# Empty places of the neighbour lists get an index past the rows, and every indexed gather carries a bound that skips them

## The chip, the cores and the metric

The kernel runs on one core of a Trainium2 chip. The metric is the device time of one execution in microseconds (us). Before the change its median over 9 runs is 2172.87 us (2168.15 to 2176.95).

The core's engines are written as in the profile: PE is TensorE (matmuls; PEld its weight loads), DVE is VectorE, ACT is ScalarE, POOL is GpSimd, SP is SyncE. SP and ACT issue plain DMAs; POOL issues the gathers by index (DMA_INDIRECT). All of them run on the same 16 DMA engines.

## The reference

Input x is 8 x 2048 x 256 and adj is 2048 x 2048, both float32. adj is sparse: 18,432 of its 4,194,304 entries are not zero (9 in a row on average, more in the first rows than in the last), and the diagonal is always filled. Two layers are computed, each with a residual and a layer norm.

```python
# layer 0: graph convolution
A_norm = A + eye(n)
deg    = sum(A_norm, 0) + sum(A_norm, 1) - diagonal(A_norm)
dinv   = rsqrt(deg)
A_hat  = A_norm * dinv[:, None] * dinv[None, :]
agg    = einsum('nm,bmd->bnd', A_hat, x).reshape(-1, d)
h      = relu(batchnorm(agg @ W1.T + b1, g1, be1))
out    = batchnorm(h @ W2.T + b2, g2, be2)
x      = layernorm(x + out)
# layer 1: attention of 4 heads, only where adj is not zero
q, k, v = split(x @ W)
scores  = q k^T / 8 + where(adj == 0, -inf, 0)
x       = layernorm(x + softmax(scores) v)
```

## The kernel before

The 2048 rows are cut into 16 blocks of 128 (one row per partition). Block 0, and in layer 0 block 1 too, is computed densely with matmuls. For the other blocks the kernel builds neighbour lists from adj and works on gathered rows.

**Lists** (`list_steps`, lines 246 to 321). For block t, `LISTS[t]` gives two numbers, such as (8, 3). The first is the number of columns in which partition p holds a neighbour of its own row p. Rows with more neighbours than that put the surplus into the left-over columns (the second number), where a partition holds any edge of the block and also the number of the row that it belongs to. In all there are 131 columns of 128 places, 35 of them left-over. `val` is 2048 minus the neighbour's number, and 0 in an empty place. Line 306 turns it into `key` = 2048 - val, line 307 limits it to 2047, so an empty place names the last row, and line 308 writes it as the integer `idx`. For the left-over columns `qi1` is the row of the edge within the block plus 1, or 0 when empty; lines 309 to 312 make of it `idxq`, the row whose query is to be gathered. Lines 313 to 319 make `fidx`, the place of the value in adj taken as one flat column: row times 2048 plus key. `padb` is -2^40 for an empty place, so that its exponential is 0, and `weights` (line 335) multiplies the weight of an empty place by 0.

Counted from the inputs, 2,352 of the 16,768 places are empty: 1,014 in the columns of a partition's own row, spread over the partitions, and 1,338 of the 4,480 left-over places, always the last partitions of the last columns.

**Layer 0.** `gather_value` (line 326) gathers one adj value per place into a column of `av`, 115 times. `gather` (line 562) gathers 128 rows of `xs_d` (x scaled by dinv, all 8 batches, 8 KB a row) into a slot, called `e` in the profile, 115 times. Sixteen slots are shared with other data; `gather_ahead` issues up to ten gathers before the tile in work. Own-row columns are added up on DVE (lines 639 and 643), left-over columns on PE with a 128 x 128 weight matrix (line 652). Between them run the first linear layer (line 393) and the list building of later blocks. A second pass (lines 680 to 812) has the second linear layer and the batch norm statistics.

**Attention** (`attention`, line 879). Batches go in four pairs. For each pair a projection writes rows of keys and values (4,128 bytes for a pair) to `kv_d` and of queries to `q_d`. Then for each of the 131 columns (blocks 1 to 15) `gather` (line 1211) gathers 128 rows into `kg` (10 buffers) and, in left-over columns, 128 query rows of 2 KB into `qg` (5 buffers). `score` multiplies and sums on DVE (lines 1233, 1235), `exps` is on ACT (1244), `weigh_values` on DVE or ACT (1265, 1260), `add_up` on PE (1276). The finished block goes through `finish` (DVE, 1087 and 1089), `residual` (POOL, 1096) and the output norm: `out_root` (two small POOL instructions, lines 144 and 146, a pow), `out_shift` (DVE, 866), `emit` (ACT, then a store on SP).

The order of every engine's instructions is written out by hand: a loop over the 524 columns of all pairs issues the score of column n + 5, the addition of column n and the gather of column n + 10, and a table `later` hangs the steps of the next pair's projection and of the norms on column numbers. The first ten gathers of the attention are issued together, at column number -19, while the first projection ends. Everything on POOL stands in one queue: gathers, residual additions, the norms' pow and memsets.

Of the kernel before, what the change touches and what calls it, by code (L numbers as in the profile page):

```python
# [14 lines left out]
ALU = mybir.AluOpType  # L15
# [27 lines left out]
def tile_gcn_then_masked_attention(  # L43
# [15 lines left out]
    nc = tc.nc  # L59
    ENG = mybir.EngineType  # L60
    PSUM = bass.MemoryType.PSUM
    P = 128
    B, N, D = x.shape
# [51 lines left out]
    qi1 = cpool.tile([P, NEDGE], F32, name="qi1")  # L115
# [130 lines left out]
    def list_steps(t, psum, name):  # L246

        r, m, cap, e0 = ELL[t], 8 * ROUNDS[t], CAP[t], edge0[t]
        here = slice(t, t + 1)
        ell = slice(col0[t], col0[t] + r)  # L250
        left_over = slice(col0[t] + r, col0[t] + r + cap)
        cols = slice(col0[t], col0[t] + r + cap)
        edges = slice(e0, e0 + cap)

        def junk():
            return lists.tile([P, MAXNB], F32, name="junk", bufs=2)

        nc.vector.scalar_tensor_tensor(
            junk()[:, : m - r], nbx[:, t, r:m], 0.0, ones[:, : m - r],
            op0=ALU.is_gt, op1=ALU.mult, accum_out=cnt[:, here],  # L260
        )
        nc.vector.tensor_copy(val[:, ell], nbx[:, t, :r])
        nc.vector.tensor_scalar(
            over[:, 0, here], nbx[:, t, m - 1 : m], 0.0, None, op0=ALU.is_gt
        )
        yield
        yield
        ps = psum.tile([P, 1], F32, name=name)
        nc.tensor.matmul(ps, tri, cnt[:, here], start=True, stop=True)
        yield  # L270
        nc.vector.tensor_copy(nbx[:, t, MAXNB : MAXNB + 1], ps)
        nc.vector.tensor_add(end[:, here], cnt[:, here], nbx[:, t, MAXNB : MAXNB + 1])
        nc.vector.tensor_scalar(
            over[:, 1, here], end[:, here], float(cap * P), None, op0=ALU.is_gt
        )
        oh = lists.tile([P, WE], F32, name="oh")[:, : cap * P]
        nc.vector.tensor_scalar(
            oh, iota_e[:, : cap * P], nbx[:, t, MAXNB : MAXNB + 1], None, op0=ALU.is_ge
        )
        nc.vector.scalar_tensor_tensor(  # L280
            oh, iota_e[:, : cap * P], end[:, here], oh, op0=ALU.is_lt, op1=ALU.mult
        )
        yield
        yield
        pg = psum.tile([P, cap, MAXNB + 2 - r], F32, name=name)
        for i in range(cap):
            nc.tensor.matmul(
                pg[:, i, :], oh[:, i * P : (i + 1) * P], nbx[:, t, r:], start=True, stop=True
            )
        yield  # L290
        rank = lists.tile([P, cap], F32, name="rank")
        nc.vector.tensor_sub(rank, epos[:, :cap], pg[:, :, MAXNB - r])
        nc.vector.tensor_copy(qi1[:, edges], pg[:, :, MAXNB + 1 - r])
        nc.vector.tensor_scalar(qn1[:, edges], qi1[:, edges], -1.0, None, op0=ALU.mult)
        for i in range(cap):
            c = left_over.start + i
            nc.vector.scalar_tensor_tensor(
                junk()[:, : m - r], iota_r[:, : m - r], rank[:, i : i + 1], pg[:, i, : m - r],
                op0=ALU.is_equal, op1=ALU.mult, accum_out=val[:, c : c + 1],
            )  # L300
        nc.vector.tensor_scalar(
            padb[:, cols], val[:, cols], 0.0, MASKED, op0=ALU.is_equal, op1=ALU.mult
        )
        key = lists.tile([P, MAXNB], F32, name="key")[:, : r + cap]
        q = lists.tile([P, cap], F32, name="q")
        nc.vector.tensor_scalar(key, val[:, cols], -1.0, float(N), op0=ALU.mult, op1=ALU.add)
        nc.vector.tensor_scalar(key, key, float(N - 1), None, op0=ALU.min)
        nc.vector.tensor_copy(idx[:, cols], key)
        nc.vector.tensor_scalar(
            q, qi1[:, edges], 1.0, float(t * P - 1), op0=ALU.max, op1=ALU.add  # L310
        )
        nc.vector.tensor_copy(idxq[:, edges], q)
        nc.vector.scalar_tensor_tensor(
            fidx[:, ell], rowid[:, here].to_broadcast([P, r]), float(N), key[:, :r],
            op0=ALU.mult, op1=ALU.add,
        )
        nc.vector.scalar_tensor_tensor(
            fidx[:, left_over], q, float(N), key[:, r:], op0=ALU.mult, op1=ALU.add
        )
        nc.vector.tensor_scalar(wgt[:, ell], key[:, :r], rowid[:, here], None, op0=ALU.is_equal)  # L320
        nc.vector.tensor_tensor(wgt[:, left_over], key[:, r:], q, op=ALU.is_equal)

    adj_flat = adj.rearrange("n (m o) -> (n m) o", o=1)
    av = lists.tile([P, NCOL], F32, name="av")

    def gather_value(col):
        nc.gpsimd.indirect_dma_start(  # L327
            out=av[:, col : col + 1], out_offset=None, in_=adj_flat,
            in_offset=bass.IndirectOffsetOnAxis(ap=fidx[:, col : col + 1], axis=0),
        )  # L330

    def on_vector(t):
# [82 lines left out]
    with tc.tile_pool(name="first", bufs=1, side="right") as fp, tc.manual_schedule(  # L415
# [5 lines left out]
        with tc.tile_pool(name="pst", bufs=4, space=PSUM) as pst, tc.tile_pool(  # L421
# [54 lines left out]
            for t in (2, 3):  # L476
                for _ in list_steps(t, pst, "ps"):
                    pass
# [40 lines left out]
    with tc.tile_pool(name="l0", bufs=1, side="right", reuse_waits="tile") as lp, tc.tile_pool(  # L519
# [42 lines left out]
        def gather(n):  # L562
            col = tiles[n][2]
            xg[n] = Slot()
            nc.gpsimd.indirect_dma_start(  # L565
                out=xg[n].t, out_offset=None, in_=xs_d[:],
                in_offset=bass.IndirectOffsetOnAxis(ap=idx[:, col : col + 1], axis=0),
            )

        def gather_ahead(n):  # L570
            keep = 2 + owed[0]
            while gathered[0] < min(n + 10, len(tiles)) and (
                len(free) > keep or gathered[0] <= n
            ):
                gather(gathered[0])
                gathered[0] += 1
# [41 lines left out]
        for n in range(len(tiles)):  # L618
            t, r, col, e, mine, k, count = tiles[n]
            for u in range(4, NT):  # L620
                if n == max(0, first[u] - VLEAD - 12):
                    making.append(list_steps(u, psh, "ph"))
            if n == first[NT - 1] - VLEAD - 12:
                assert next(search, None) is None and not rows_of
                making.append(list_steps(1, psh, "ph"))
# [4 lines left out]
            if first[4] <= v < len(tiles):  # L630
                gather_value(tiles[v][2])
# [4 lines left out]
            if mine:  # L636
# [5 lines left out]
                else:  # L642
                    nc.vector.scalar_tensor_tensor(  # L643
                        agr[t].t, xg[n].t, wgt[:, col : col + 1], agr[t].t,
                        op0=ALU.mult, op1=ALU.add,
# [233 lines left out]
    def attention():  # L879

        with ExitStack() as st:
# [314 lines left out]
            LEAD = 10  # L1196
            AHEAD = 5
            ON_ACT, LAST_ON_ACT = (1, 3), (0, 2, 4)
            kg, qg, qb, oh, sc, pw, wv, po = ({} for _ in range(8))

            def load_q(k):

                p, t = k // (NT - 1), k % (NT - 1) + 1
                if p == NP:
                    return
                qb[p, t] = ep.tile([P, G2, D], F32, name="qb", bufs=3)
                nc.sync.dma_start(
                    qb[p, t].rearrange("p b d -> p (b d)"), q_d[p][t * P : (t + 1) * P, :]
                )

            def gather(n):
                p, g = divmod(n, NG)
                t, r, col, e = tiles[g]
                kg[n] = ep.tile([P, G2, KW], F32, name="kg", bufs=LEAD)
                nc.gpsimd.indirect_dma_start(  # L1215
                    out=kg[n].rearrange("p b e -> p (b e)"), out_offset=None, in_=kv_d[p][:],
                    in_offset=bass.IndirectOffsetOnAxis(ap=idx[:, col : col + 1], axis=0),
                )
                if e >= 0:
                    qg[n] = ep.tile([P, G2, D], F32, name="qg", bufs=5)  # L1220
                    nc.gpsimd.indirect_dma_start(  # L1221
                        out=qg[n].rearrange("p b e -> p (b e)"), out_offset=None, in_=q_d[p][:],
                        in_offset=bass.IndirectOffsetOnAxis(ap=idxq[:, e : e + 1], axis=0),
                    )

            def score(n):
# [82 lines left out]
            for n in range(min(later), 0):  # L1309
                side_tasks(n)  # L1310
                if n == GATHER:
                    for k in range(2):
                        load_q(k)
                    for m in range(LEAD):
                        gather(m)
# [6 lines left out]
            for n in range(NALL_G):  # L1322
                p, g = divmod(n, NG)
                t, r, _, _ = tiles[g]
# [26 lines left out]
            for n in sorted(later):  # L1351
# [7 lines left out]
                ok, flat, INV_MAX, ok, op0=ALU.is_le, op1=ALU.mult, accum_out=cnt[:, 0:1],  # L1359
# [238 lines left out]
    def attention_with_maxima():  # L1598

        with tc.tile_pool(name="full", bufs=2) as ap_, tc.tile_pool(  # L1600
# [10 lines left out]
            for b in range(B):  # L1611
# [55 lines left out]
                for c in range(NCH):  # L1667
# [3 lines left out]
                    for half in range(2):  # L1671
                        inp.emit(b, c, half)

    attention()


# [47 lines left out]
```

## Time and profile before

| what | value |
|---|---|
| median of 9 runs | 2172.87 us |
| profiled execution | 2175.39 us |
| its span in the profile | 2173.7 us |
| PE, DVE, ACT, POOL busy | 1928.5, 1736.6, 1379.7, 1434.5 us |
| gathers: kg, qg, e, av | 524, 140, 115, 115 |
| their mean time on POOL | 1067, 1018, 1411, 1362 ns |
| queue q0 (the gathers) | 106,896 packets, 434.28 MB, 53.4% of 16 engines' span |
| queue q1 (SP's) | 149,968 packets, 228.96 MB, 29.9% |

The busy time of a gather on POOL is the time in which POOL writes its descriptors; the rows land later (median 7.5 us after the start for kg, 7.1 for qg, 10.2 for e, 7.9 for av). A line of a group or of a wait names the line of the kernel, the engine, and the tile that is written, an arrow, and the tiles that are read; buffer numbers are left out. A line of the waits has the waiting instruction, an arrow, what ended the wait, the sum in us, how often, and the longest. "issue" is idle time in which nothing that the profile shows was waited for. In the table of stretches each engine has its busy us in the stretch and the number of its instructions, then come the granted TensorE clock, the mean busy share of the DMA engines, and GB/s.

### The profile page before, as it was taken

Reading aid. Unit: us, or ns where it says so; the run is one execution under the profiler, and the core shown is the slowest. Engines: PE = TensorE matmul, PEld = TensorE weight load, DVE = VectorE, ACT = ScalarE, POOL = GpSimd, SP = SyncE. Lnnn points to the kernel's source line nnn. Section 1 sums busy time; section 2 is a strip of 40 time slices with the busy share of each in tenths; the row PEclk is TensorE's granted clock in tenths of the full one; section 3 lists DMA queues with packets and bytes.
Section 4 is the critical chain, followed back from the end, with each engine's and each line's share of the span. In section 5 each row is a group of like instructions: output and inputs, shape, how many; then the busy total and the mean of one; then the engine's idle time right before and its main releaser. Section 6 shows DMA issues by size and latency. Waiting matters only on the chain.

```text
span 2173.7 us, 27900 instructions
## 1 busy us (share of the span) xinstructions
PE 1928.5 (89%) x7590; PEld 1258.6 (58%) x7590; DVE 1736.6 (80%) x3537; ACT 1379.7 (63%) x4145; POOL 1434.5 (66%) x1417
## 2 busy tenths in 40 slices
PE   5599978899999996989999999999999999788784
PEld 1244444445434444657776776777777677666673
DVE  6862898889856663239899998899998999988896
ACT  6222322223355544658888887878888887799886
POOL 2322688888457761136777786777886777878874
PEclk7699989999999998989999999999999999999987
DMA  8598999999838526578999998999999999999994
GB/s 319 192 305 345 419 353 373 348 386 394 321 100 295 172 83 210 189 265 329 337 373 334 347 347 329 359 334 354 338 357 355 340 356 351 371 355 368 333 354 159
DMA packets 259335, 681.89 MB, mean 314 GB/s; under 512 B 25952, under 2 KB 125024, under 8 KB 234208
## 3 DMA queue, kind: packets, MB, share of 16 engines
q0 software_dynamic: 106896, 434.28, 53.4%
q1 hardware_dynamic: 149968, 228.96, 29.9%
q10 hardware_dynamic: 2304, 16.78, 1.8%
q8 instruction: 63, 1.03, 0.2%
q14 instruction: 104, 0.85, 0.1%
HBM read 553.31 MB, written 126.62 MB: 313 GB/s over the span
## 4 chain that ended last, share of the span: by engine, by line
PE 48%; DVE 19%; ACT 14%; DMA 9%; issue 6%; POOL 4%; SPq 0%; DVEq 0%; ACTq 0%; POOLq 0%
PE pm L1000 9%; PE pa L721 8%; PE po L1276 7%; PE ph L393 7%; ACT wv L1260 7%; PE pa L493 5%; DMA x<-in_x_dram 4%; DVE pr L1233 4%; PE pa L652 3%; DVE s L1235 3%; ACT x L872 3%; DVE wv L1265 2%; DVE e L643 2%; PE pm L1049 2%; PE po L1068 2%
## 5 line engine op out<-in xcount | busy, mean ns | idle before, releaser
L1215 POOL DMA_INDIRECT kg<-kv_d,idx x524 | 559.0, 1067 | 146.4 <-issue 81.6
L1260 ACT ACTIVATE wv<-kg,pw 128x65 f32<-128x65 f32 x1880 | 473.4, 336 | 0.3 <-PE po L1276 0.3
L1276 PE MATMUL po<-wv,ident 128*128 128x260 f32 x1536 | 435.2, 396 | 40.3 <-DVE z L1089 38.1
L1235 DVE TENSOR_REDUCE s<-pr 128x8 f32<-128x512 f32 x524 | 359.3, 686 | 34.5 <-DVE pr L1233 0.5
L1000 PE MATMUL pm<-wq,x1t 128*128 128x512 f32 (+1 forms) x1024 | 375.0, 497 | 12.2 <-ACT x1t L945 12.2
L1276 PEld LDWEIGHTS po<-wv,ident 128*128 128x128 f32 x1536 | 286.6, 196 | 104.1 <-issue 56.4
L1233 DVE TENSOR_TENSOR pr<-qb,kg 128x512 f32<-128x512 f32 x384 | 273.4, 712 | 9.7 <-DMA kg<-kv_d,idx 7.2
L1000 PEld LDWEIGHTS pm<-wq,x1t 128*128 128x128 f32 x1024 | 186.8, 193 | 104.8 <-issue 73.5
L565 POOL DMA_INDIRECT e<-xs_d,idx x115 | 162.3, 1411 | 119.6 <-DMA xs_d<-xt 63.0
L1244 ACT ACTIVATE pw<-s,padb 128x8 f32<-128x8 f32 x524 | 155.3, 298 | 131.7 <-DVE s L1235 130.6
L393 PE MATMUL ph<-e,w1s 128*128 128x512 f32 x512 | 226.8, 594 | 0.8 <-ACT e L398 0.8
L1265 DVE TENSOR_TENSOR wv<-kg,pw 128x520 f32<-128x520 f32 x289 | 208.9, 723 | 2.3 <-PE po L1276 1.6
L327 POOL DMA_INDIRECT av<-in_adj_dram,fidx x115 | 156.7, 1362 | 46.6 <-issue 31.7
L1276 PE MATMUL po<-wv,oh 128*128 128x260 f32 x560 | 174.4, 397 | 2.0 <-DVE wv L1265 1.3
L1221 POOL DMA_INDIRECT qg<-q_d,idxq x140 | 142.5, 1018 | 42.7 <-issue 41.8
L643 DVE SCALAR_TENSOR_TENSOR e<-e,wgt,e 128x2048 f32<-128x2048 f32 x70 | 163.8, 2340 | 0.2
L398 ACT ACTIVATE h<-ph,b1s 128x512 f32<-128x512 f32 x96 | 66.0, 687 | 154.1 <-PE ph L393 141.0
L393 PEld LDWEIGHTS ph<-e,w1s 128*128 128x128 f32 x512 | 95.6, 190 | 113.7 <-issue 110.2
L1068 PEld LDWEIGHTS po<-kvr,p 128*128 128x128 f32 x1024 | 138.9, 199 | 37.0 <-ACT p L1057 27.2
L1068 PE MATMUL po<-kvr,p 128*128 128x65 f32 x1024 | 135.8, 278 | 22.4 <-ACT p L1057 22.2
L1096 POOL TENSOR_TENSOR x<-z,x 128x256 f32<-128x256 f32 x126 | 125.1, 994 | 44.4 <-DVE z L1089 42.5
L1049 PE MATMUL pm<-q,kt 128*128 128x256 f32 x512 | 136.5, 390 | 10.3 <-ACT kt L1037 4.8
(193 smaller groups left out, 3295.4 us busy)
## 6 DMA issues: line engine op xcount, KB each, us to landing
kv_d<-kvr SPq DMA_DIRECT2D x32, 1032.0 KB, 7.3
h_d<-h SPq DMA_DIRECT2D x24, 1024.0 KB, 9.0
e<-h_d SPq DMA_DIRECT2D x24, 1024.0 KB, 6.5
e<-in_adj_dram SPq DMA_DIRECT2D x16, 1024.0 KB, 18.7
xt<-in_x_dram SPq DMA_DIRECT2D x16, 1024.0 KB, 7.1
xs_d<-xt ACTq DMA_DIRECT2D x16, 1024.0 KB, 6.7
y_d<-y SPq DMA_DIRECT2D x128, 128.0 KB, 2.2
yt<-y_d SPq DMA_DIRECT2D x32, 512.0 KB, 10.4
```

The costliest lines, as they stand in the source:

```text
L393: nc.tensor.matmul(ph, w1s[:, d, f * P : (f + 1) * P], as_agb(agb[t])[:, d, r * B // 2 : (r + 1) * B // 2, :], start=(d == 0), stop=(d == ...
L643: nc.vector.scalar_tensor_tensor(agr[t].t, xg[n].t, wgt[:, col : col + 1], agr[t].t, op0=ALU.mult, op1=ALU.add,)
L721: nc.tensor.matmul(py, w[:, f, :], t[:, f, :], start=(f == 0), stop=(f == 1))
L1000: nc.tensor.matmul(pm, x1t[b, c][:, d, i * P : (i + 1) * P], rhs(d), start=(d == 0), stop=(d == ND - 1),)
L1049: nc.tensor.matmul(pm[:, hp].rearrange("p r q -> p (r q)"), k[:, hp, :], q0[b][:, hp].rearrange("p r q -> p (r q)"), start=False, stop=Tru ...
L1068: nc.tensor.matmul(po0[b][:, h, :], p[:, h, :], heads(kvr[b, c][:, i, D:])[:, h, :], start=(j == 0 and h == 0), stop=(j == NT - 1), skip_g ...
L1215: nc.gpsimd.indirect_dma_start(out=kg[n].rearrange("p b e -> p (b e)"), out_offset=None, in_=kv_d[p][:], in_offset=bass.IndirectOffsetOnAx ...
L1233: nc.vector.tensor_mul(pr, q, kg[n][:, :, :D])
L1235: nc.vector.tensor_reduce(s.rearrange("p b h -> p (b h)"), pr.rearrange("p b (h e) -> p (b h) e", e=HD), AX.X, ALU.add,)
L1260: nc.scalar.activation(wv[n][:, b, hs], k[:, b, D:][:, hs], AF.Copy, scale=w[:, b, h : h + 1],)
L1265: nc.vector.tensor_mul(wv[n].rearrange("p b (h e) -> p b h e", e=VW), k[:, :, D:].rearrange("p b (h e) -> p b h e", e=VW), w[:, :, :, None ...
L1276: nc.tensor.matmul(po[p, t, b].rearrange("p h e -> p (h e)"), oh[n] if e >= 0 else ident, wv[n][:, b, :], start=(r == 0), stop=(r == ELL[t ...
```

## The change

Line 307 goes: `key` is 2048 in an empty place, one past the last row. An empty left-over place gets a query row past the end too: 4096 is added where `qi1` is 0. Every indexed gather now carries a bound, the last valid index, with `oob_is_err=False`: a place whose index is above the bound is not transferred, and its destination keeps what it held. So that this is a finite number, `av` is cleared once (on POOL), and the ten `kg` and five `qg` buffers are cleared by DVE before their first gather. In the program the bound is in a register; one register move stands on POOL ahead of each of the 894 gathers. No other instruction is added, removed or moved on any engine.

```diff
         nc.vector.tensor_scalar(key, val[:, cols], -1.0, float(N), op0=ALU.mult, op1=ALU.add)
-        nc.vector.tensor_scalar(key, key, float(N - 1), None, op0=ALU.min)
         nc.vector.tensor_copy(idx[:, cols], key)
         nc.vector.tensor_scalar(
-            q, qi1[:, edges], 1.0, float(t * P - 1), op0=ALU.max, op1=ALU.add
+            q, qi1[:, edges], 0.0, float(2 * N), op0=ALU.is_equal, op1=ALU.mult
+        )
+        nc.vector.scalar_tensor_tensor(
+            q, qi1[:, edges], float(t * P - 1), q, op0=ALU.add, op1=ALU.add
         )
...
     av = lists.tile([P, NCOL], F32, name="av")
+    nc.gpsimd.memset(av, 0.0)
...
             in_offset=bass.IndirectOffsetOnAxis(ap=fidx[:, col : col + 1], axis=0),
+            bounds_check=N * N - 1, oob_is_err=False,
...
                 in_offset=bass.IndirectOffsetOnAxis(ap=idx[:, col : col + 1], axis=0),
+                bounds_check=N - 1, oob_is_err=False,
...
+            filled = []
...
                 kg[n] = ep.tile([P, G2, KW], F32, name="kg", bufs=LEAD)
+                if n < LEAD:
+                    nc.vector.memset(kg[n], 0.0)
...
                     in_offset=bass.IndirectOffsetOnAxis(ap=idx[:, col : col + 1], axis=0),
+                    bounds_check=N - 1, oob_is_err=False,
...
                     qg[n] = ep.tile([P, G2, D], F32, name="qg", bufs=5)
+                    if len(filled) < 5:
+                        filled.append(n)
+                        nc.vector.memset(qg[n], 0.0)
...
                         in_offset=bass.IndirectOffsetOnAxis(ap=idxq[:, e : e + 1], axis=0),
+                        bounds_check=N - 1, oob_is_err=False,
```

## The prediction

> **What bounds the kernel now.** I read the table of stretches first, because the page's shares average stages with different limits.
>
> ```profile
> core 0: us, PE busy (x) PEld busy (x) DVE busy (x) ACT busy (x) POOL busy (x), PEclk, DMA share, GB/s
> 205.00:440.00 235.00, 202.39 (x571) 102.53 (x570) 203.34 (x416) 61.09 (x95) 174.75 (x123) 0.92 0.97 374
> 440.00:562.00 122.00, 121.97 (x368) 60.09 (x367) 111.53 (x218) 39.30 (x63) 100.37 (x71) 0.99 0.97 381
> ...
> 1550.00:1850.00 300.00, 287.75 (x1378) 221.67 (x1378) 279.25 (x550) 250.18 (x866) 230.12 (x264) 0.99 0.95 352
> 1850.00:2130.00 280.00, 223.84 (x1058) 181.16 (x1056) 254.00 (x469) 248.75 (x934) 225.50 (x227) 0.92 0.96 351
> ```
>
> The first two stretches are the gathers of layer 0, the last two belong to the attention. TensorE is full from 440 to 562 us and nearly so until 1850; in the tail (1850 to 2130) it is at 80% and VectorE carries most. The DMA engines look full (0.95 to 0.97), so fewer bytes seem the obvious gain. The waits of VectorE say how much that can be:
>
> ```profile
> DVE lo_nm L866 <- POOL lo_rs L146: 17.2, 14, 2.7
> DVE x L916 <- DMA x<-in_x_dram: 11.9, 4, 4.9
> DVE pr L1233 <- DMA kg<-kv_d,idx: 7.2, 10, 1.5
> DVE pr L1233 <- DMA qg<-q_d,idxq: 6.4, 10, 1.2
> ```
>
> In the whole attention VectorE stood 13.6 us for gathered rows and 11.9 for loads of x; in layer 0 it stood 11.2 for the value gather. So 36.7 us, 1.7% of the span, is all that VectorE loses to transfers that a lighter queue could speed up. TensorE has no wait for a gather in these stages.
>
> Then the queue that issues the gathers, in the tail:
>
> ```profile
> POOL kg L1215 <- issue: 20.4, 80, 0.3
> POOL qg L1221 <- issue: 10.7, 35, 0.3
> ...
> 2003.05 0.95 POOL L1221 DMA_INDIRECT qg<-q_d,idxq  x1 [0.30 <-issue]
> 2004.30 1.45 POOL L1215 DMA_INDIRECT kg<-kv_d,idx  x1 [0.30 <-issue]
> 2006.06 1.09 POOL L1215 DMA_INDIRECT kg<-kv_d,idx  x1 [0.30 <-DVE s L1235]
> ```
>
> POOL's 66% on the page hides that each gather is preceded by 0.30 us in which nothing is awaited. The tail holds 134 kg and 36 qg gathers; 225.5 busy and 170 x 0.305 = 52 make 277 of 280 us. Idle time beyond that 0.31 us (gaps after other instructions counted as they are) is POOL's **slack**. Summed from the trace by stretch it is 24.6 us (205 to 440), 0.3 (440 to 562), 64.8 (930 to 1250), 31.6 (1250 to 1550), 26.8 (1550 to 1850) and 8.5 in the tail. The change touches every gather, so what it does to POOL counts at full price where slack ends, and what it does to bytes counts only against 36.7 us.
>
> **The change part by part.**
>
> *Skipped bytes.* From the inputs, 2,352 of 16,768 listed places are empty (14.0%, 18 of a gather's 128), and of the 4,480 places that have a gathered query 1,338 (30%, 38 of 128). Tables and row sizes give 39 MB of kg, 11 of qg and 18 of e, 67 of the software queue's 434 MB (15%). The gathers' landings (median 7.5 us for kg) should shorten by at most that share, 1.1 us. Today a gather with few filled places lands no later than a full one (median 6.7 us under 16 filled, 7.1 with 128), so the repeated last row is no hot spot whose end would give more. VectorE's waits for kg and qg last 0.7 us on average, so those outside the tail go (7.5 us); in the tail (6.1) the gathers are issued later, see below. The waits for x and the values lose 15%, 3.5 us. Sum -11. A rule of the Trainium skill (DMA: Bandwidth & Descriptors, section Anatomy of one DMA) puts a transfer at 2.0 us and its bytes over 436 GB/s. By it a kg landing is 3.2 us, not the 7.5 measured with many in flight, and 14% of its variable 1.2 us is 0.17 us; the relief would then be about -3 instead of -11.
>
> *The gather instruction.* It gets a bound in a register, one register move ahead of each of the 894 gathers. Sequencer work in that place is free: the 0.30 us stand whether no, one, two or three semaphore instructions lie between two gathers (304 to 306 ns each), so the move (29 to 39 ns in its two occurrences) costs 0; uncovered it would be 664 x 0.034 = 23 us of POOL in the attention. The bound itself has no row. All four gathers take 0.93 to 0.95 us at best, with rows of 4 bytes or 8 KB, so the price goes by indices: 0.94 / 128 = 7.3 ns. Bounds: a skipped index costs nothing, then a kg gather saves 18 x 7.3 ns = 0.13 us; or the test doubles every index, then it costs 0.94 us more. I take a value near the gather's own row: kept indices as now, a skipped one twice, because it is read and compared like any and then leaves the straight path. That is +0.13 us for kg and e, 38 x 7.3 ns = +0.28 for qg, +0.08 for the value gather (only its left-over columns skip: an empty place of the other columns gives row x 2048 + 2048, which lies inside adj except for the last row).
>
> A rule that speaks against the change: the Trainium skill (GPSIMD Engine Reference, section 3.1 Elementwise) has data-dependent branching at about 12 cycles an element, 10 ns at the 1.2 GHz it uses, or 1.28 us for 128 indices. No row here shows it; by it, on every index, the time would pass 2800 us.
>
> With my value: tail 134 x 0.13 + 36 x 0.28 = 27.5, less 8.5 slack, **+19**. 1550 to 1850: 130 x 0.13 + 35 x 0.28 = 26.7 against 26.8, 0. 1250 to 1550: 25.3 against 31.6, and 930 to 1250: 26.7 against 64.8, 0. 205 to 440: 64 x 0.13 + 59 x 0.08 = 13 against 24.6, 0. 440 to 562: 38 x 0.13 + 32 x 0.08 = 7.5 against 0.3, but there the gathered rows lay ready 6 to 18 us before they were read, so 0; without that cover +7. Queued behind the gathers on POOL are the pow of the 30 output norms, for which VectorE already waits (the lo_nm row): 30 x 0.13 = +4.
>
> *Memsets.* Ten of 128x1032 and five of 128x512 on VectorE, and one of 128x131 on POOL ahead of the first adj rows, hidden by that load (5 us). No row has a VectorE memset; the 128x2048 rows with one and with two inputs (1354 and 2340 ns) bound 1032 columns by 0.68 and 1.18 us, and I take the lower. The ten and two of the five stand where VectorE sits idle from 937 to 959 us (22.0 us, waiting for PE pm); they need 7.5, at most 13. The first gather, at 937.8, moves back by 0.7; its reader starts at 965. If that idle were gone they would cost the 7.5. Three stand in the loop: +1.
>
> *Lists.* One small VectorE instruction goes and one comes in each of 15 lists, 0.17 us each: 0.
>
> Sum: +19 + 4 + 1 - 11 = **+13 us**. The profiled execution took 2175.4 us (span 2173.7), 2.5 above the median; I add to the median: 2172.9 + 13 = **2186 us**.
>
> **The rivals.** *A*, the forecast: a skipped index is dearer than a kept one. With 1.3 times its price POOL's extra falls within slack and relief rules (about 2165); with 2.5 times it is 41 in the tail, less 8.5, 13 and 6 in the two stretches before, 6 for the norms, 3 in layer 0, less 8: 2225. So 2165 to 2225.
>
> *B*, the other side: a skipped index costs POOL nothing. Then POOL frees 27.5 us in the tail, the gathers are early, all 13.6 us of VectorE's waits for rows go, 3.5 of x and values, and a quarter of 20 for the norms: -22 + 1, so 2152 (2140 to 2158). More is not there: in the tail VectorE has 254 busy and 13 in gaps below 150 ns of 280. It decides where skipping is cheaper than keeping. For it: no descriptors need be written. Against: the issue time today does not depend on the bytes.
>
> *C*: kept and skipped cost the same; relief alone, 2160.
>
> *D*: every index pays the test. From 8.5 / 170 = 0.05 us a gather the tail stretches. At 0.3: 42 in the tail, 23 and 15 before it, 15 in layer 0, 9 for the norms, less 5: 2272. At the upper bound, 0.94: about 2815.
>
> *E*, the change does not do what it says: a skipped place is still fetched, as most empty values are. No relief, no price: 2174.
>
> **How the numbers follow.** This kernel's times tell 0.2% from no change, so the border is 2168.5 and 2177.2. A 0.42 (0.33 slower, 0.09 same), B 0.22 faster, C 0.10 (0.08 faster, 0.02 same), D 0.20 slower, E 0.06 same. Faster 0.30, same 0.17, slower 0.53. The range 2142 to 2265 leaves out most of D (0.16) and the low end of B (0.02).
>
> **What would show it.** Right: kg's median issue 0.96 us now to about 1.09, qg's to 1.23, the emptiest gathers slowest, the 0.30 us unchanged; packets of q0 15% fewer; slack of the tail gone and VectorE's waits for kg there grown. A kg issue near 0.83 says B, the same for full and empty gathers above 1.2 says D, unchanged packets say E. It would be wrong altogether if VectorE's or TensorE's own durations moved, or if the memsets held up what follows 959 us.

## The result and the profile after

The changed kernel takes 2184.7 us (median of 10 runs, 2182.5 to 2188.5) against 2172.3 (33 runs): a ratio of 1.0057 [1.0047, 1.0067], 12.4 us more. The forecast was 2186, or +13. The total is right; the place where it arises, and the price that it was worked out from, are not.

The profiled execution took 2184.8 us (span 2183.0; before 2173.7, so 9.3 of the 12.4 us are in this pair of traces). I cut both spans at the first and last matmul of the first linear layer (lines 393 and 397) and at the first score of the attention:

| stretch, us | before | after | difference | forecast for it |
|---|---|---|---|---|
| up to layer 0's first linear matmul | 204.2 | 202.2 | -2.0 | 0 |
| layer 0, first to last of them | 411.2 | 422.1 | **+10.9** | -1.7 (15% of 11.2) |
| second linear, first projection | 349.4 | 350.8 | +1.4 | 0 |
| attention | 1208.8 | 1207.9 | **-0.9** | +14.7 (19 + 4 + 1 - 7.5 - 1.8) |

The first row is scatter: in the traces of all runs below it lies between 202.2 and 203.7 us, and a second trace of the same code as before up to there (number 8) has 202.2.

The four pairs of the attention went from 300.5, 314.7, 299.9 and 293.7 us to 300.9, 310.0, 300.3 and 296.8.

The first view after is the table of stretches:

```profile
core 0: us, PE busy (x) PEld busy (x) DVE busy (x) ACT busy (x) POOL busy (x), PEclk, DMA share, GB/s
205.00:440.00 235.00, 196.99 (x557) 99.57 (x555) 200.09 (x407) 59.10 (x91) 186.21 (x119) 0.91 0.88 327
440.00:562.00 122.00, 118.01 (x344) 59.04 (x345) 105.47 (x214) 37.46 (x59) 102.20 (x66) 0.96 0.86 308
1850.00:2130.00 280.00, 227.05 (x1059) 182.13 (x1057) 254.35 (x468) 246.03 (x924) 229.62 (x227) 0.91 0.89 308
```

In these stretches the DMA share fell by 0.07 to 0.11, GB/s by 12 to 19%. In layer 0 this was not enough to help: POOL has 11.5 us more busy time in the first row, and TensorE, full before in the second row (121.97 of 122), now has 4 us of gaps. In the tail the engines stand as they stood. The waits of VectorE, in the attention (four lines) and in layer 0 (the last two, before and after):

```profile
DVE lo_nm L871 <- POOL lo_rs L146: 19.3, 16, 2.8
DVE pr L1246 <- DMA kg<-kv_d,idx: 6.5, 9, 1.4
DVE x L921 <- DMA x<-in_x_dram: 3.5, 2, 2.1
DVE pr L1246 <- DMA qg<-q_d,idxq: 3.4, 5, 1.2
```

```profile
DVE wgt L339 <- DMA av<-in_adj_dram,fidx: 11.2, 3, 5.2
DVE wgt L343 <- DMA av<-in_adj_dram,fidx: 24.1, 4, 6.9
```

In the attention the waits for transfers fell from 25.5 to 13.4 us (kg 7.2 to 6.5, qg 6.4 to 3.4, x 11.9 to 3.5), as the step on bytes had it. (Each is one profiled execution; the two other first-series runs with the changed attention, numbers 2 and 4, have 17.8 and 17.6, and number 3, with the attention of before, 23.3.) In layer 0 the wait for gathered adj values, which the forecast had put among those to shrink, went from 11.2 to 24.1: +12.9, and the stretch is 10.9 longer. The gathers themselves, by tile (minimum, median and maximum in ns); first before, then after:

```profile
L1215 POOL DMA_INDIRECT kg<-kv_d,idx x524: 932/958/1600, 937.8 to 2139.2; - x175
L1221 POOL DMA_INDIRECT qg<-q_d,idxq x140: 947/953/1453, 941.7 to 2138.0; - x140
L327 POOL DMA_INDIRECT av<-in_adj_dram,fidx x115: 940/949/3048, 83.2 to 546.5; - x115
```

```profile
L1223 POOL DMA_INDIRECT kg<-kv_d,idx x524: 986/1012/1658, 947.6 to 2148.2; - x175
L1233 POOL DMA_INDIRECT qg<-q_d,idxq x140: 999/1006/1521, 951.7 to 2146.7; - x140
L330 POOL DMA_INDIRECT av<-in_adj_dram,fidx x115: 992/1002/3161, 83.4 to 563.4; - x115
```

All rose by the same 52 to 54 ns in the minimum, and by 53 to 62 in the median. It does not matter how many places are skipped: qg, which skips 38 of 128 on average, rose as much as kg, which skips 18, and kg gathers with all 128 places filled have the minimum of 986 ns, those under 16 filled 1002. The gap ahead of a gather stayed at 305 ns (median), and the register move (29 ns) lies in it.

The queue of the gathers and the whole:

```profile
DMA packets 259342, 614.67 MB, mean 282 GB/s; under 512 B 40171, under 2 KB 139243, under 8 KB 236351
q0 software_dynamic: 106896, 366.99, 47.9%
```

The packets of q0 are the same 106,896 to the last one, but 67.3 MB are gone, the 67 worked out in the forecast, and packets under 512 bytes rose from 25,952 to 40,171. Among those of q0 there are 11,551 more of 4 bytes and 2,668 new ones of 8, while those of 4,128 bytes fell by 9,408: four pairs times the 2,352 empty places. So a skipped place still makes a packet, of 4 bytes instead of a row (8 where two query rows shared one).

### The profile page after: what moved, and what is told of

Same layout as the page of the kernel before. It is cut to its first block, busy times and chain, and to the rows that moved or that the text cites. A ratio compares the mean times of both kernels' runs of the same rounds, so it can differ in the third digit from the quotient of the medians.

```text
span 2183.0 us, 28819 instructions
## 1 busy us (share of the span) xinstructions
PE 1927.4 (88%) x7590; PEld 1258.6 (58%) x7590; DVE 1751.9 (80%) x3552; ACT 1381.7 (63%) x4145; POOL 1489.6 (68%) x1418
## 3 DMA queue, kind: packets, MB, share of 16 engines
q0 software_dynamic: 106896, 366.99, 47.9%
HBM read 553.31 MB, written 126.62 MB: 311 GB/s over the span
## 4 chain that ended last, share of the span: by engine, by line
PE 45%; DVE 21%; ACT 14%; DMA 8%; issue 7%; POOL 4%; SPq 0%; DVEq 0%; POOLq 0%; ACTq 0%
PE pm L1005 9%; PE pa L726 8%; PE ph L397 7%; ACT wv L1273 6%; PE po L1289 6%; PE pa L497 5%; DVE pr L1246 5%; PE pa L657 3%; DVE s L1248 3%; DVE wv L1278 3%; ACT x L877 3%; DMA e<-in_adj_dram 2%; PE pm L1054 2%; DMA qg<-q_d,idxq 2%; POOL kg L1223 2%
## 5 line engine op out<-in xcount | busy, mean ns | idle before, releaser
L1223 POOL DMA_INDIRECT kg<-kv_d,idx x524 | 590.9, 1128 | 142.7 <-issue 84.1
L1246 DVE TENSOR_TENSOR pr<-qb,kg 128x512 f32<-128x512 f32 x384 | 278.4, 725 | 9.9 <-DMA kg<-kv_d,idx 6.5
L569 POOL DMA_INDIRECT e<-xs_d,idx x115 | 174.3, 1516 | 109.8 <-DMA xs_d<-xt 61.5
L330 POOL DMA_INDIRECT av<-in_adj_dram,fidx x115 | 173.0, 1504 | 43.6 <-issue 30.5
L1233 POOL DMA_INDIRECT qg<-q_d,idxq x140 | 147.6, 1054 | 47.7 <-issue 38.7
L1101 POOL TENSOR_TENSOR x<-z,x 128x256 f32<-128x256 f32 x126 | 118.0, 938 | 32.4 <-DVE z L1094 30.0
```

The source lines that it names most:

```text
L569: nc.gpsimd.indirect_dma_start(out=xg[n].t, out_offset=None, in_=xs_d[:], in_offset=bass.IndirectOffsetOnAxis(ap=idx[:, col : col + 1], ax ...
L1223: nc.gpsimd.indirect_dma_start(out=kg[n].rearrange("p b e -> p (b e)"), out_offset=None, in_=kv_d[p][:], in_offset=bass.IndirectOffsetOnAx ...
L1246: nc.vector.tensor_mul(pr, q, kg[n][:, :, :D])
```

## Experiments

**Theories.** "Flat": the bound adds about 0.05 us to the issue of every gather whatever its indices; skipping neither costs nor saves POOL time; attention has the slack and the relief to pay it, layer 0's POOL has no slack where it matters, and loses. "Skip", the forecast's: a skipped index costs about 7 ns more than a kept one, and the tail pays. A third one had to be told apart in layer 0: that not POOL's time but something else of the bounded gathers (their landing, their packets) delays the values.

The runs form three series, numbers 1 to 4, 5 to 8 and 9 to 12. Each is compared with runs of the kernel before in the same series (medians 2174.6, 2191.1 and 2192.2 us); the change, in the second row, with those of the result. The three last columns come from one profiled execution, whose time lies up to 5.6 us from the median of its row. Layer 0 varies little there (410.7 to 413.0 us in the five traces without a bound in it), the attention more.

| run | us | ratio, 95% | layer 0, us | attention, us | wait for av, us |
|---|---|---|---|---|---|
| the kernel before | 2172.3 | 1 | 411.2 | 1208.8 | 11.2 |
| the change | 2184.7 | 1.0057 [1.0047, 1.0067] | 422.1 | 1207.9 | 24.1 |
| bound only | 2198.2 | 1.0117 [1.0102, 1.0131] | 425.4 | 1215.4 | 32.6 |
| attention only | 2173.6 | 1.0002 [0.9992, 1.0012] | 413.0 | 1205.3 | 14.6 |
| layer 0 only | 2187.8 | 1.0064 [1.0049, 1.0079] | 422.6 | 1209.0 | 30.5 |
| values unbounded | 2179.4 | 1.0023 [1.0011, 1.0035] | 414.4 | 1211.4 | 11.9 |
| attention, left-over only | 2185.9 | 0.9968 [0.9955, 0.9981] | 411.1 | 1219.1 | 14.0 |
| change, values earlier | 2195.4 | 1.0015 [0.9998, 1.0032] | 423.7 | 1219.4 | 19.2 |
| before, values earlier | 2190.8 | 0.9991 [0.9975, 1.0006] | 410.7 | 1220.1 | 6.3 |
| the change again | 2194.8 | 1.0016 [1.0000, 1.0032] | 422.4 | 1215.0 | 23.1 |
| POOL load, no bound | 2208.5 | 1.0079 [1.0058, 1.0101] | 426.1 | 1220.1 | 21.9 |
| left-over only, values earlier | 2185.9 | 0.9973 [0.9957, 0.9989] | 411.3 | 1215.8 | 8.1 |
| change, values earlier, again | 2195.8 | 1.0015 [1.0000, 1.0031] | 425.1 | 1213.1 | 22.0 |

**1. The bound without skipping** (`e1_bound_only`): before's lists, in which no index is past the rows, and the bound on all four gathers.

```diff
             in_offset=bass.IndirectOffsetOnAxis(ap=fidx[:, col : col + 1], axis=0),
+            bounds_check=N * N - 1, oob_is_err=False,
...
+                bounds_check=N - 1, oob_is_err=False,
```

> All gathers carry the bound, the lists are those of before, so no place is skipped and the output is whole. Flat theory (the bound itself adds about 0.05 us to the issue of every gather, skipped places cost what kept ones do): shortest issue of kg 0.986 us as in the changed kernel, layer 0 some 11 us longer than before, the tail longer too because no transfer gets lighter; 12 to 25 us over before, ratio 1.006 to 1.012. Skip theory (the prediction: a skipped index costs twice a kept one, the bound nothing): issue as before (0.932), time within 2 us of before, ratio 0.999 to 1.001.

Nothing is skipped here, and the gathers cost the same as in the changed kernel:

```profile
L1217 POOL DMA_INDIRECT kg<-kv_d,idx x524: 984/1013/1657, 950.6 to 2159.3; - x175
```

"Skip" falls with this line. The run is also slower than the change, 1.0117 against 1.0057. The difference, 0.006 x 2173 = 13 us, is what skipping the bytes brings back, the memsets that it needs paid (by the table 3.3 of it lie in layer 0 and 7.5 in the attention).

**2. Attention only** (`e2_attention_only`): layer 0 as before; three VectorE instructions ahead of the attention move the empty places past the rows; bounds and memsets in the attention.

```diff
+            nc.vector.scalar_tensor_tensor(idx, padb, 0.0, idx, op0=ALU.is_lt, op1=ALU.add)
+            nc.vector.tensor_scalar(qz, qi1, 0.0, float(2 * N), op0=ALU.is_equal, op1=ALU.mult)
+            nc.vector.tensor_tensor(idxq, qz, idxq, op=ALU.add)
```

> Layer 0 as before; bound, skipped places and memsets in the attention alone (three small VectorE instructions move the indices past the rows between the layers). Flat theory: layer 0 back to before, the attention's extra 37 us of POOL repaid by shorter landings: 2 us below to 2 us above before, ratio 0.999 to 1.001. Skip theory: the tail pays 19 us and the norms 4, relief gives 11 back: about 12 us over before, ratio 1.004 to 1.007.

No difference, 1.0002 [0.9992, 1.0012]. In this series price and relief cancel in the attention.

**3. Layer 0 only** (`e3_layer0_only`): the change without its attention part; `idx` and `idxq` are brought back to the rows before it.

```diff
+            nc.vector.tensor_scalar(idx, idx, float(N - 1), None, op0=ALU.min)
+            nc.vector.tensor_scalar(idxq, idxq, float(N - 1), None, op0=ALU.min)
...
-                    bounds_check=N - 1, oob_is_err=False,
```

> Bound and skipped places in layer 0 alone; the attention's gathers are unbounded with the limited index, no memsets of kg and qg. Flat theory: the whole loss is here, 9 to 13 us over before, ratio 1.004 to 1.006. Skip theory: covered in layer 0, and lighter transfers: 0 to 4 us below before, ratio 0.998 to 1.000.

1.0064 [1.0049, 1.0079], layer 0 422.6: the whole loss is here.

**4. Values unbounded** (`e4_values_unbounded`): the change, but the gathers of adj values have no bound, and their list is limited to the last place by one small VectorE instruction.

```diff
+        nc.vector.tensor_scalar(fidx[:, cols], fidx[:, cols], float(N * N - 1), None, op0=ALU.min)
...
-            bounds_check=N * N - 1, oob_is_err=False,
```

> The changed kernel, but the 115 value gathers carry no bound (their places are limited to the last element of adj by one more small VectorE instruction per list, 15 x 0.17 us). They save 460 bytes each at most, so the bound there is pure price. Flat theory with POOL's queue as the place of the loss: 115 x 0.054 = 6 us of POOL and the stalls that go with it leave layer 0, about half of the 12 us: ratio to before 1.001 to 1.004. If layer 0 loses by its row gathers or by VectorE's own lists instead: as the changed kernel or slower, 1.005 to 1.008.

The ratio is 1.0023 [1.0011, 1.0035]. Layer 0 fell from 422 to 414.4 us, and the wait for the values is back at its old size:

```profile
DVE wgt L342 <- DMA av<-in_adj_dram,fidx: 11.9, 6, 6.6
```

**5. Forms of a value gather** (`e5_value_forms`): seven forms in turn, for their issue times alone.

```diff
+        elif turn[0] % 7 == 3:
+            nc.gpsimd.indirect_dma_start(
+                out=av[:64, col : col + 1], out_offset=None, in_=adj_flat,
+                in_offset=bass.IndirectOffsetOnAxis(ap=fidx[:64, col : col + 1], axis=0),
+                bounds_check=N * N - 1, oob_is_err=False,
+            )
```

> One look. The kernel before, but its 115 value gathers take turns in seven forms, each on its own line: 128, 64 and 32 places without and with the skipping bound, and 128 with a bound that would report an error. All indices are in range. With 64 and 32 places the other adj values are left at zero, so this part of the weights is left out. If the bound is tested index by index, its price falls with the places: 0.052 us at 128, 0.026 at 64, 0.013 at 32. If it is a price per instruction (fetching the bound), it stays near 0.052 at all three. The bound that reports errors costs the same as the skipping one if the price is that of the bound, nothing if it is that of the skipping.

The lines are, in this order: 128 places with the skipping bound; 64 without and with it; 32 without and with it; 128 with a bound that reports an error; 128 without:

```profile
L337 POOL DMA_INDIRECT av<-in_adj_dram,fidx x17: 997/1011/3088, 83.7 to 545.3; - x17
L343 POOL DMA_INDIRECT av<-in_adj_dram,fidx x17: 915/920/3010, 89.2 to 546.6; - x17
L348 POOL DMA_INDIRECT av<-in_adj_dram,fidx x17: 962/972/2119, 90.5 to 549.0; - x17
L354 POOL DMA_INDIRECT av<-in_adj_dram,fidx x16: 878/886/2160, 91.7 to 530.4; - x16
L359 POOL DMA_INDIRECT av<-in_adj_dram,fidx x16: 917/934/3026, 92.9 to 532.9; - x16
L365 POOL DMA_INDIRECT av<-in_adj_dram,fidx x16: 1037/1814/2852, 96.2 to 535.9; - x16
L332 POOL DMA_INDIRECT av<-in_adj_dram,fidx x16: 945/967/2443, 97.6 to 540.7; - x16
```

By the minima (the medians also hold issues that something delayed), 96 more places cost 945 - 878 = 67 ns, 0.7 ns each, over a fixed 0.86 us. The bound costs 52 ns at 128 places, 47 at 64 and 39 at 32: an estimate of 35 ns for the instruction and 0.13 ns for a place. The medians without and with the bound (967 and 1011, 920 and 972, 886 and 934) put it at 44, 52 and 48 ns, with no trend, so the part that goes by places is at most small. Each form has 16 or 17 gathers of one execution.

**6. Bound only where much is empty** (`e6_attention_left_over`): layer 0 as before; in the attention only the left-over columns (30% empty) are skipped and bounded, 140 kg and 140 qg gathers of 664.

```diff
+                bound = {} if e < 0 else dict(bounds_check=N - 1, oob_is_err=False)
...
+                    **bound,
```

> Bound and skipped places only in the attention's left-over columns (140 kg and 140 qg gathers, 30% of their places empty); everything else as before. Flat theory: 280 x 0.054 = 15 us of POOL instead of 37, with 33 of the attention's 50 MB still saved: 1 to 6 us below before, ratio 0.997 to 0.9995. If the attention's result was the skipping's own work and not a balance of POOL and relief: as with the bound on all of the attention, 0.999 to 1.001.

0.9968 [0.9955, 0.9981]: faster than the kernel before. 280 gathers instead of 894 pay, 30% of their places are skipped, and layer 0 is untouched (411.1). That the choice of columns makes the gain is not shown: the bound on the whole attention (number 2) was not run in this series, and here the kernel before is itself slower (see what stays open). By the change, 1.0057 in the first series and 1.0016 in the third, number 2 would move from 1.0002 to an estimated 0.996, which is as low.

**7 and 8. Values earlier** (`e7_after_values_earlier`, `e8_before_values_earlier`): the value gathers are issued two columns earlier, in the changed kernel and in the kernel before.

```diff
-        VLEAD, making = 16, []
+        VLEAD, making = 18, []
```

> The changed kernel with its value gathers issued 18 tiles ahead and not 16 (lists too). If layer 0 loses because a POOL queue without slack delivers the values late to the weights (VectorE's wait for av 24 us against 11), two tiles more lead take 6 to 10 us of the loss back: ratio to before 1.000 to 1.004. If POOL's throughput bounds the whole of layer 0, lead changes nothing: 1.004 to 1.007.

> Control: the kernel before with the same 18 tiles of lead. If the lead acts on the wait for values, at most the 11 us that VectorE waits there are to be had: ratio 0.995 to 0.999. If POOL's throughput bounds layer 0: 0.999 to 1.001.

The ratio of number 7, 1.0015 [0.9998, 1.0032], taken alone falls in the range of "late values". But the change without the lead has 1.0016 in the third series (number 9), so the lead took nothing off, and the layer 0 of number 7 stays long (423.7). VectorE's wait for the values is still 19.2 us, and TensorE now waits for gathered rows as well:

```profile
PE pa L657 <- DMA e<-xs_d,idx: 8.6, 4, 3.4
```

The kernel before has no such wait. So it is not one gather's place in the queue but the queue's throughput. With the lead the kernel before gains nothing that can be told either (0.9991, number 8).

**9. The change again** (`e9_changed_again`), beside the runs that follow.

> The changed kernel itself, on the chip of the other runs of this call, so that they can be compared with it: ratio to before 1.0047 to 1.0067 as measured first.

1.0016 [1.0000, 1.0032] here, not 1.0057 as expected. Layer 0 lost what it had lost (422.4), so the rest of the kernel, 2.6 us over before in all, must have gained some 8 us. The traces point to the attention: 1215.0 us, where number 10, whose attention is that of before, has 1220.1 in the same series; see what stays open.

**10. POOL load without a bound** (`e10_pool_load`): the kernel before, with four memsets of 128x4 on POOL ahead of each of the 230 gathers of layer 0.

```diff
+        for i in range(4):
+            nc.gpsimd.memset(load[:, 4 * i : 4 * i + 4], 0.0)
         nc.gpsimd.indirect_dma_start(
```

> The kernel before, no bound anywhere; only four small memsets (128x4) on POOL ahead of each of layer 0's 230 gathers, as heavy a load as the bound (four such memsets and the shorter gap after them take some 0.06 us more than the gap that a gather has now). If the loss of layer 0 is POOL's throughput and nothing else about the bound: layer 0 is 9 to 15 us longer, ratio 1.004 to 1.007. If the skipped places or the bounded transfers themselves hurt: within 0.1% of before.

POOL's timeline (start, duration, instruction, idle time before it) shows what the load amounts to:

```profile
470.53 0.22 POOL L329 MEMSET load<- 128x4 f32 x4
470.90 0.96 POOL L330 DMA_INDIRECT av<-in_adj_dram,fidx  x1 [0.15 <-issue]
471.86 0.22 POOL L569 MEMSET load<- 128x4 f32 x4
472.23 1.72 POOL L570 DMA_INDIRECT e<-xs_d,idx  x1 [0.15 <-issue]
```

From the end of one gather to the start of the next it is 0.372 us instead of 0.305, 0.067 more, and the gathers' minima are 13 ns above those of before: 0.080 us for each gather, half as much again as the bound. Layer 0 took 426.1 us, 15 more, and the wait for values 21.9. POOL time alone is enough to make the loss; the third theory isn't needed. It also gives its rate. 230 x 0.080 = 18 us of load cost 15; 230 x 0.054 = 12.4 cost 14 in experiment 1 and, with the bytes skipped, 11 in the change; in experiment 4, where only the rows are bounded and skipped, 115 x 0.054 = 6.2 cost 3. So where no bytes are saved beside it, about as much as is added to POOL in all arrives in layer 0. This is a rate and not a chain of cause: 36 of the 230 gathers start before 205 us, where POOL does not hold layer 0 up.

**11 and 12.** The left-over form with values earlier (`e11_left_over_and_lead`), and number 7 once more (`e12_values_earlier_again`).

> The bound only in the attention's left-over columns, and layer 0 unbounded with its value gathers 18 tiles ahead: the two versions that did not lose, together. If their gains add: 0.994 to 0.997. If the lead does nothing: as the left-over version alone, 0.9955 to 0.998.

> The changed kernel with 18 tiles of lead once more, beside the changed kernel on the same chip. If POOL's throughput bounds layer 0, its ratio is that of the changed kernel within 0.001, since what the values gain the rows lose. If the lead matters it is 0.002 to 0.004 below the changed kernel.

0.9973 [0.9957, 0.9989] repeats the gain of number 6; the two columns of lead add nothing to it. 1.0015 [1.0000, 1.0031], number 9's ratio within 0.001, as the theory of POOL's throughput has it (layer 0 425.1, the wait for values 22.0). The lowest ratios are those of numbers 6 and 11.

## Why the prediction was right and wrong

**Right.** The move costs nothing (gap 0.305 us before and after). Skipping relieves the transfers by the bytes worked out: kg lands after 6.5 us instead of 7.5 (at most 1.1 was said; medians of the 330 and 194 gathers whose landing the traces tell), qg 6.5 instead of 7.1, and the relief of -11 stands beside 13 in experiment 1 against the change. The estimate that the fit in the Trainium skill (DMA: Bandwidth & Descriptors, Anatomy of one DMA) gave, -3, is too small: the landings of kg here shortened by 1 us and not by 0.17. The memsets took 918 ns each for kg, between the bounds 0.68 and 1.18, and the first gather stands 0.9 us later against layer 0's end (0.7 was said). The norms' wait rose from 17.2 to 19.3, +2 instead of +4.

**Wrong: "the price goes by indices: 0.94 / 128 = 7.3 ns", and "a skipped one twice".** That all four gathers took the same time with rows of 4 bytes or 8 KB showed that the price does not go by bytes. It did not show that it goes by indices, since all gathers had 128. Experiment 5 varied them: 0.7 ns an index over 0.86 us. With a tenth of the price per index (0.7 ns for 7.3), neither "dearer" nor "cheaper than keeping" could be large; rival B had the same root. The bound is a flat 0.054 us. Of the rivals D is nearest, since every gather pays, at a sixth of the 0.3 it was priced at and right at the point from which it was said to decide; but D had every index pay, and most of the price goes by the instruction.

The estimate from the Trainium skill's figure for data-dependent branching (GPSIMD Engine Reference, section 3.1 Elementwise; 1.28 us for 128 indices) is 24 times the 0.052 us that the bound cost at 128 places in experiment 5, so that figure does not carry over to this test.

**Wrong: the tail "+19".** With the measured price the forecast's own sum gives 170 x 0.054 - 8.5 = +0.7. The last pair took 3.1 us more, and the second pair 4.7 less.

**Wrong: layer 0 "0", for want of the right cover.** The sum put 7.5 us of issue time (440 to 562 us) against 0.3 us of slack, and let it go because the gathered rows lay ready 6 to 18 us before they were read. That was the cover of one of the two products of the queue. The adj values stand in the same queue. In the trace of before three blocks waited for theirs (1.4, 4.6 and 5.2 us); for five that did not, the trace tells when the last value landed: 5.3, 2.5, 0.2, 0.6 and 7.2 us before the weights were computed. The forecast showed that very wait, 11.2 us, and counted only its relief.

**Wrong: layer 0 "0", for slack that lies elsewhere.** From 205 to 440 us the sum put 13 us against 24.6 us of slack. The trace of before, with that stretch cut in two at 260 us (columns as in the table of stretches):

```profile
205.00:260.00 55.00, 52.60 (x155) 26.11 (x153) 47.83 (x93) 16.92 (x27) 26.64 (x22) 0.97 1.01 418
260.00:440.00 180.00, 149.79 (x419) 76.42 (x418) 155.51 (x324) 44.17 (x68) 148.11 (x102) 0.90 0.96 361
```

Until 260 us POOL is busy for 26.64 of 55 us. After that, 148.11 us and 101 gaps of 0.305 us make 179 of 180. Of the slack 23.6 us lie in the first row and 1.1 in the second. So POOL is full from 260 us on and not from 440, and it issues 171 gathers until 562 us with 1.4 us of slack. At the measured price that is 171 x 0.054 - 1.4 = 7.8 us, more than half of it ahead of 440 us, where the forecast had 0. Its "without that cover +7" counted 70 gathers at a dearer price and is near 7.8 by chance. Layer 0 lost 10.9 us; 5.1 of them had come by the row addition that starts at 440 us before. How the 3 us beyond 7.8 arise is not shown; the gathers that stand behind a VectorE instruction cost POOL 13 us more than before (below).

With the flat price, but with layer 0 left at 0, the sum would have been +0.7 + 1.6 (30 norms x 0.054) + 1 - 11 = -8. That the total was right is luck: two errors of opposite sign met, by the first table 15.6 us too much in the attention and 12.6 too little in layer 0.

**A marker badly chosen.** "Packets of q0 15% fewer" and "unchanged packets say E" both failed, while the skip works: bytes tell it, packets do not.

## What to carry to other kernels

A bound on an indexed gather is paid for by every gather and brings back bytes only where places are empty: weigh the two for each group of gathers, and keep it off those whose issuing queue has no slack. Equal durations of equal instructions say nothing of what they scale with; vary the size before pricing a part of it. For a queue that feeds several readers, take the margin of each of its products in the stretch in question, and take the shortest. And look where in a stretch the slack lies before setting a cost against its sum.

## What was not expected, and what stays open

**Issues that stand behind a VectorE instruction.** In layer 0 some gathers' issues take 2 to 3 us. The timeline of the changed kernel, first VectorE's two-input instruction on rows (128x2048), then POOL:

```profile
469.95 2.35 DVE L648 SCALAR_TENSOR_TENSOR e<-e,wgt,e 128x2048 f32<-128x2048 f32 x1
...
474.57 2.35 DVE L648 SCALAR_TENSOR_TENSOR e<-e,wgt,e 128x2048 f32<-128x2048 f32 x1
...
478.04 2.33 DVE L648 SCALAR_TENSOR_TENSOR e<-e,wgt,e 128x2048 f32<-128x2048 f32 x1
```

```profile
470.20 2.97 POOL L330 DMA_INDIRECT av<-in_adj_dram,fidx  x1 [0.30 <-issue]
473.48 0.99 POOL L569 DMA_INDIRECT e<-xs_d,idx  x1 [0.31 <-issue]
474.77 3.02 POOL L330 DMA_INDIRECT av<-in_adj_dram,fidx  x1 [0.30 <-DMA e<-xs_d,idx]
478.10 3.13 POOL L569 DMA_INDIRECT e<-xs_d,idx  x1 [0.30 <-issue]
```

A gather that starts while this instruction runs ends 0.87 us after it ends: 470.20 + 2.97 = 473.17 against 472.30, then 477.79 against 476.92, and 481.23 against 480.37. From 205 to 562 us it is so for 61 gathers before (0.81 to 0.87 us, median 0.81) and for 62 after (0.86 to 0.88, median 0.87; the 0.05 of the bound once more); seven more that started within 0.01 us of the instruction (six before, one after) were not held. Against the median of the others these gathers cost POOL 85 us before and 98 after. The one-input instruction on the same rows (line 639, 128x2048) holds gathers too: all eight that start while it runs in the trace of before end 0.80 to 0.84 us after it. The 39 of that trace that start during a batch norm statistic (128x512) take 0.94 us in the median, no longer than the others. The Trainium skill (SBUF — State Buffer, section SBUF: two separate sides) says that VectorE and GpSimd share a port pair as a lock, and that GpSimd cannot write the descriptors of its DMAs while VectorE holds it in an operation of its two-port mode, with a float32 copy as the example; an operation with two inputs in SBUF holds it too, but only against a GpSimd operation that reads SBUF. The trace agrees in that gathers, which read their indices from SBUF, are held by a one-input and by a two-input instruction; that it is the port which holds them is the page's account, and no run here shows it. This is how layer 0's POOL comes to be full with a quarter of its time (98 of 357 us) spent waiting. This was read off the traces alone: no run shortened that VectorE instruction.

**Open: the kernel before is 0.8% slower in the second and third series** (2191 and 2192 us against 2173 to 2175), with layer 0 the same (411 us in the runs that leave it alone) and the attention longer (1213 to 1220 us in the table, 1205 to 1215 in the first series). There the rest of the kernel gains more from the change, so that it costs 1.0016 and not 1.0057. The traces show one place: VectorE's waits ahead of `wv` in the attention sum to 0.7 to 3.1 us in the first series and to 6.5 to 19.8 us in the second and third, with the bound and without it. The cause was not found; the record has the first two series on the same chip, so the chip alone is not it. Ratios were therefore compared within a series only, and which of numbers 2 and 6 is the faster stays open.

**Open: the bytes read.** The page counts 553.31 MB read from memory before and after, though q0 moved 67 MB less. No run tells why. Why a bound that reports an error costs 92 ns, and not 52, is open too.
